# Two fused layers on one core: a norm pinned behind a multiplication, mixer factors issued sooner, down products moved, the last silu in halves

## The chip, the core and the metric

The kernel runs on one core of a Trainium2 chip. The metric is the device time of one execution in microseconds (us). Engines are named as the profile names them: PE (TensorE, matmuls) with PEld (its weight loads), DVE (VectorE), ACT (ScalarE), POOL (GpSimd) and SP (SyncE, which issues nearly all DMAs). Each engine works through its own queue in order, so an instruction that waits holds back all that stand behind it on that engine.

## What is computed

Four batches of 512 tokens with 256 features pass through two layers. Both layers compute `x + s * silu(ffn(xn))` with `xn = layernorm(x)`:

```
def ffn(x, W1, W2, W3):                 # H = 1024 hidden features
    hidden = silu(x @ W1.T) * (x @ W3.T)
    return fwht(hidden) @ W2.T          # fwht: normalised Hadamard transform
layer 0: s = xn + rmsnorm(mix(xn)) * norm_w      # mix starts from a zero state
layer 1: s = attention(layernorm(xn) * gamma + beta) + xn   # causal, one head
x = x + s * silu(ffn(xn))
```

Since the state of `mix` starts at zero, it is a linear map: the factors of B and C are summed to one number per feature, `g`, and `W_out`, `g` and `W_in` are multiplied to one 256x256 matrix `m` on the chip. The Hadamard transform is applied to W2 once per layer.

## The kernel before, in words

**Products.** All large products are made in three passes: each operand is split into a high part (a cast on ACT, line 61) and the rest (a subtraction on DVE, line 62), and PE multiplies high with high, high with low and low with high. `split` (line 59) is this pair of instructions. All matmuls go through line 70. In the profile, names ending in h and l are the two parts.

**Banks.** PE's results lie in eight PSUM banks in three groups: `gu` (3 banks), `dn` (2) and `ms` (3). A tile that is asked for takes the bank of its group that was given out longest ago, and its first product waits until the last reader of the former tile is done.

**Layer 0.** For each batch `ffn` (line 446) goes over eight chunks of 128 hidden features: two up products (`gu`, lines 484 to 502), silu on ACT (505), multiplication on DVE (506), a split (513). One chunk later `down` (456) multiplies by the transformed W2 into the two `dn` banks, which are given out at the start of `ffn` (452). Beside the chunks a list of background steps runs (`Beside`, line 832; each step ends at a `yield`). In batch 0 they are `prep_first` (919): the butterflies and products that transform W2 (`prep_w2`, 139), and `prep_m` (204), which makes `g` on DVE (lines 207, 209, 211), scales `W_out` by it on ACT (`wg`, line 214, four instructions), and multiplies (`mps`) to `m`; then the mixer (670). The order of the instructions in layer 0 is set by a planner that simulates a timeline before the run. `after(ins)` puts what is issued inside it behind `ins` on the same engine; it makes no wait between engines.

**Layer 1.** PE's order is written out by hand (`line["fixed"]`, line 1020): each matmul follows the one issued before it. The other engines are still planned. `ffn_s` (530) goes over four pairs of chunks, q = 0 to 3. For each it makes seven block products (Strassen's scheme) of six matmuls each, in the order gate, z, gate, z, gate, lin, gate, in three `gu` banks (`gate_`, `lin`, `z`). Between them stand eight places, filled from the list `places` by the caller (lines 1035 to 1063): steps of the attention (`sc`, `pt`, `pv`, `tq`, `v`), and numbers 0 to 3, which are the down products of the pair before: 0 and 1 for tokens 0 to 255 with the first and second chunk of the pair, 2 and 3 for tokens 256 to 511. `silu(h1)`, line 626 and a split make the hidden values of the first 256 tokens; `silu(h0)` (631), the multiplication at line 632 and a split (634 to 636) those of the other 256. Line 632 is the last reader of the pair's `lin` bank.

The next norm: at the last place of pair 3 of batches 0 and 1 the caller takes the first step of `norm(1, b + 2)` (412): means and variances on DVE (259, 261, 263), the power -1/2 on POOL (264), the scaling on DVE (266). It is issued inside `after(first["gate"])` (line 415); `first["gate"]` is, at that point, line 619 of the same pair, the addition to `v`. The second step, the moments of the normed values (`mr`, 243 to 248, again with a power on POOL), is issued at place 2 of the first pair of the next batch; at its place 7 PE transposes them (`mrp`) and they go to DRAM and back (`mrb`).

**The last batch.** Its down products for tokens 256 to 511 need two banks of `ms` beside the attention, so some of them stand as tuples in `places` (`later`, line 1058): `(q, chunk, (2, 3))` for tiles 2 and 3 of 128 tokens. What is left runs in the loop at 642, 36 matmuls, and `gate_tile` (1001) ends each tile with silu (1004), two DVE steps (1005, 1006) and a DMA (1007).

Of the kernel before, what the change touches and what calls it, by code (L numbers as in the profile page):

```python
# [17 lines left out]
ALU = mybir.AluOpType  # L18
# [17 lines left out]
def kernel(ctx: ExitStack, tc: tile.TileContext, a: dict, out: bass.AP):  # L36
# [142 lines left out]
    def product_of_weights(name, lhsT, rhs, nk, scale=None):  # L179

        hi = wp.tile([P, 2, D], F32R, name=f"{name}h")
        lo = wp.tile([P, 2, D], F32R, name=f"{name}l")
        o = psum(f"{name}ps", [P, 2, D])
        for i in range(2):
            for k in range(nk):
                matmul(
                    o[:, i, :], lhsT(k, i), rhs(k), start=k == 0, stop=k == nk - 1
                )
        if scale is None:
            split(o, hi, lo)  # L190
        else:
            nc.scalar.mul(hi, o, scale)
            nc.vector.scalar_tensor_tensor(lo, o, scale, hi.bitcast(F32), ALU.mult, ALU.subtract)
        return hi, lo
# [9 lines left out]
    def prep_m(win, wout):  # L204

        cb = wp.tile([P, 4, 2, DS], F32, name="cb")
        nc.vector.tensor_tensor(cb, bc[:, :, 0:2, :], bc[:, :, 2:4, :], ALU.mult)
        cbd = wp.tile([P, 4, DS], F32, name="cbd")
        nc.vector.tensor_tensor(cbd, cb[:, :, 0, :], cb[:, :, 1, :], ALU.subtract)
        g = wp.tile([P, 4], F32, name="g")  # L210
        nc.vector.tensor_reduce(g, cbd, AX.X, ALU.add)
        wg = t4("wg", [P, 4, D])
        for c in range(4):
            nc.scalar.mul(wg[:, c, :], wout[:, c, :], g[:, c : c + 1])
        return product_of_weights(
            "m", lambda k, i: win[:, k, i * P : (i + 1) * P], lambda k: wg[:, k, :], 4
        )

    def sl(i):
        return slice(i * P, (i + 1) * P)  # L220
# [60 lines left out]
        ]  # L281

    DN = {"tag": "dn", "bufs": 2}, {"tag": "ms", "bufs": 3}
    ALLS = slice(0, S)
    ALLD = slice(0, D)

# [159 lines left out]
    def ffn(name, xT, w13, w2, slot, defer=1, spare=(), parts=1, behind=False, tail=()):  # L446

        w2h, w2l = w2
        dn = [psum(f"{name}dn{i}", [P, 2, D], tag="dn", bufs=2) for i in range(2)]
        outs = [dn[t // 2][:, t % 2, :] for t in range(NT)]
        firsts = {}

        def down(c, hh, hl, tiles=range(NT)):
            for t in tiles:
                o = outs[t]
                for n, (l, r) in enumerate(((hh, w2h), (hh, w2l), (hl, w2h))):
                    first = c == 0 and n == 0  # L460
                    stop = c == NH - 1 and n == 2

                    def one(start):
                        return matmul(
                            o, l[:, sl(t)], r[:, c, :], start=start, stop=stop, skip_group_check=True
                        )

                    if first and t % 2 == 1:  # L470
                        with tc.issue_after(firsts[t // 2].ins):
                            ins = one(False)
                    elif first:
                        ins = firsts[t // 2] = one(True)
                    else:
                        ins = one(False)
            return ins

        queue, gates = [], []
        for c in range(NH):  # L480
            with after(gates[-2] if behind and c >= 2 else None):
                wh, wl = w13(c // 2)
            gu = []
            for j in range(2):
                o = psum(f"{name}gu{c}_{j}", [P, S], tag="gu", bufs=3)
                cols = slice((c % 2) * D + j * P, (c % 2) * D + (j + 1) * P)
                gu.append((o, cols))
            for half in range(parts if c == 0 else 1):
                n = S // (parts if c == 0 else 1)
                ts_ = slice(half * n, (half + 1) * n)  # L490
                if parts == 1 or c:
                    for o, cols in gu:
                        last_up = mm3(o[:, ts_], k_pairs((wh, wl), cols, xT, ts_))
                    continue

                for n, (w, x) in enumerate(((wh, xT[0]), (wl, xT[0]), (wh, xT[1]))):
                    for o, cols in gu:
                        for k in range(2):
                            last_up = matmul(
                                o[:, ts_], w[:, k, cols], x[:, k, ts_],  # L500
                                start=n + k == 0, stop=n + k == 3,
                            )
            gu = [o for o, _ in gu]
            h = hid(f"{name}h{c}")
            first["silu"] = nc.scalar.activation(h, gu[0], AF.Silu)  # L505
            gates.append(nc.vector.tensor_tensor(h, h, gu[1], ALU.mult))  # L506
            first["gate"] = gates[-1]
            if c < len(spare):
                hh, hl = spare[c]
            else:  # L510
                hh = hid(f"{name}hh{c}", F32R)
                hl = hid(f"{name}hl{c}", F32R)
            split(h, hh, hl)
            queue.append((c, hh, hl))
            ups = last_up if behind else None
            with after(gates[-1] if behind else None), after(ups):
                slot(2 * c)
            if len(queue) > defer:
                down(*queue.pop(0))
            with after(gates[-1] if behind else None), after(ups):  # L520
                slot(2 * c + 1)
        line["fixed"] = bool(tail)
        line["last"] = last_up
        for what in tail:
            what()
        for q in queue:
            down(*q)
        return dn

    def ffn_s(name, b, pairs, w2, beside, before, last=None):  # L530
# [45 lines left out]
        for q in range(NH // 2):  # L576
# [51 lines left out]
            split(h1, *hs[0])  # L628
            place(6)
            product(gate_, A22, T4, end=True)  # L630
            silu(h0, gate_)
            nc.vector.tensor_tensor(h0, h0, lin, ALU.mult)

            left.append(run(split, h0, *hs[1]))
            if q:
                left.pop()()
            hidden[q] = hs
            place(7)
            behind = units(q, hs)
        if last is None:  # L640
            return behind, dns
        for q, t in ((2, 2), (2, 3), (3, 0), (3, 1), (3, 2), (3, 3)):
            for c in range(2):
                down(q, c, hidden[q], (t,))
            if q == 3:
                last(t, outs[t])

    def gate(name, dn, s, x, store=None, halves=range(2)):
# [270 lines left out]
    def prep_first():  # L919
        steps = prep_w2(0, raw2, w2, x_slot)  # L920
        with after(first["w13"][1]):
            next(steps)
        yield
        for _ in range(4):
            next(steps)
            yield
        with after(first["silu"]):
            nc.scalar.copy(had, had_f)
        for _ in range(4):
            next(steps)  # L930
            yield
        load_x(1)
        first["m"] = prep_m(*raw_m)
        yield
        yield from steps

# [86 lines left out]
    for b in range(B):  # L1023
# [14 lines left out]
        if not final:  # L1038
            if b:
                places[0][2].append(run(next, norms[b + 1]))  # L1040
            places[0][7].append(run(next, norms[b + 1]))
            c = Attention(b + 1)
            tq, v_ = [run(c.tq, j) for j in range(2)], [run(c.v, 0, j) for j in range(2)]
            atts.append(c)
            places += [
                [[sc[2]], [sc[3], a.soft], [0], [pts[0]], [1, later_gates[0]], [pts[1], later_gates[1]], [2], [pv[0], pv[1], 3]],
                [
                    [pts[2]], [run(c.xt_half, 0)], [0, run(c.xt_half, 1), c.xt], [pv[2]],
                    [1, c.scaled], [pv[3]], [2, c.split_sums], [3],
                ],  # L1050
                [[tq[0]], [tq[1]], [0], [v_[0]], [1], [v_[1]], [2], [3]],
            ]
            if b + 2 < B:
                norms[b + 2] = norm(1, b + 2)
                places[3][7].append(run(next, norms[b + 2]))
            behind, dn = ffn_s(f"f1_{b}", b, pairs(b), w2_1, places, behind)
        else:
            later = [[(q, c, (2, 3)) for c in range(2)] for q in range(2)]
            places += [
                [[sc[2]], [sc[3], a.soft], [0], [pts[0]], [1, later_gates[0]], [pts[1], later_gates[1]], [], [pv[0], pv[1]]],  # L1060
                [[pts[2]], [pv[2], later[0][0]], [0], [pv[3]], [1], [later[0][1]], [], []],
                [[later[1][0]], [], [0], [], [1], [later[1][1]], [], []],
            ]
            ffn_s(f"f1_{b}", b, pairs(b), w2_1, places, behind, last=gate_tile)

# [67 lines left out]
```

## Time and profile before

| | |
|---|---|
| median of 3 runs | 368.06 us (367.82 to 368.28) |
| the profiled execution | 367.46 us |
| its span in the trace | 365.6 us |
| busy PE, DVE, ACT | 97%, 78%, 54% of the span |
| granted TensorE clock | 0.999 |
| layer 0, batch 0 | starts at 0, its products at 7.81 us |
| layer 1, first pair of batches 1 and 2 (z) | 222.43 and 270.59 us |
| start of the last matmul | 361.40 us |
| end of the last DVE step, issue of the last DMA | 363.1 and 363.13 us |

Times in the profile are counted from the start of the span. In a row of the timeline stand the start, the duration, the engine, the line, the operation, output and inputs with the shape, and in brackets how long the engine stood idle before it and which instruction ended that. In a row of waits stand the sum in us, how often, and the longest. A matmul of 256 columns lasts 0.28 us but the next one starts 0.12 us after it, so rows of PE overlap.

### The profile page before, as it was taken

The page shows a single profiled execution, that of the slowest core. Times are in us where ns is not written, and L with a number is a line of the kernel's source. Part 1 is how long each engine was busy: PE and PEld are TensorE (multiplying, and loading weights), DVE is VectorE, ACT ScalarE, POOL GpSimd, SP SyncE. Part 2 cuts the span into 40 slices and gives each one's busy share as a digit, 9 for nine tenths or more (in the row PEclk, how much of TensorE's full clock was granted, in tenths as well). Part 3 has the DMA queues.
Part 4 walks back from the last instruction along what each step waited for, and adds up shares of the span by engine and source line. Part 5 has one row for each costly group of instructions (what it writes and reads, how often), then busy time and mean ns, then how long its engine had stood idle before and what let it go on. Part 6 is the DMA issues. An engine that isn't in the chain of part 4 may idle for free.

```text
span 365.6 us, 6255 instructions
## 1 busy us (share of the span) xinstructions
PE 354.9 (97%) x2461; PEld 328.3 (90%) x2461; DVE 284.5 (78%) x600; ACT 195.9 (54%) x368; POOL 20.7 (6%) x22
## 2 busy tenths in 40 slices
PE   8999999999999999999999998999989999999995
PEld 6777998888988898889999998999989999999894
DVE  6998468997579938998787967989778897588445
ACT  4655427165363425663476744576555676556343
POOL 1000111100020210101100011000020000000000
PEclk9999999999999999999999999999999999999999
DMA  7925000405144326633065324761454635545301
GB/s 226 340 69 220 3 0 2 133 39 197 63 150 172 140 47 232 241 100 104 1 244 217 117 98 191 259 240 34 189 203 166 221 135 201 189 147 194 133 2 57
DMA packets 16284, 52.25 MB, mean 143 GB/s; under 512 B 1632, under 2 KB 7936, under 8 KB 16256
## 3 DMA queue, kind: packets, MB, share of 16 engines
q1 hardware_dynamic: 15968, 51.60, 39.9%
q8 instruction: 19, 0.31, 0.4%
q10 hardware_dynamic: 288, 0.26, 0.2%
q14 instruction: 9, 0.07, 0.1%
HBM read 42.40 MB, written 9.45 MB: 142 GB/s over the span
## 4 chain that ended last, share of the span: by engine, by line
PE 81%; DVE 10%; ACT 2%; DMA 2%; issue 2%; SPq 1%; POOL 1%; DVEq 0%
PE f_2dn L70 6%; PE f_1gu L70 6%; PE f_2gu L70 6%; PE f_3gu L70 6%; PE f_0dn L70 6%; PE f_1dn L70 6%; PE f_3dn L70 4%; PE sc L70 4%; PE pv L70 3%; PE o L70 3%; PE tq L70 3%; DMA w13raw<-in_w 2%; PE v L70 2%; PE pt L70 1%; PE mps L70 1%
## 5 line engine op out<-in xcount | busy, mean ns | idle before, releaser
L70 PE MATMUL f_3gu<-xt,w 128*128 128x512 f32 x96 | 25.0, 396 | 0.0
L70 PE MATMUL f_0gu<-xt,w 128*128 128x512 f32 (+1 forms) x108 | 24.5, 380 | 0.4 <-ACT f_0h L505 0.4
L70 PE MATMUL f_2gu<-xt,w 128*128 128x512 f32 x96 | 24.6, 395 | 0.0
L70 PE MATMUL f_1gu<-xt,w 128*128 128x512 f32 x96 | 24.4, 395 | 0.0
L70 PEld LDWEIGHTS f_0gu<-xt,w 128*128 128x128 f32 x108 | 18.4, 188 | 5.2 <-issue 1.0
L70 PEld LDWEIGHTS f_1gu<-xt,w 128*128 128x128 f32 x96 | 17.2, 188 | 3.3
L70 PEld LDWEIGHTS f_2gu<-xt,w 128*128 128x128 f32 x96 | 17.1, 188 | 3.2
L70 PEld LDWEIGHTS f_3gu<-xt,w 128*128 128x128 f32 x96 | 17.0, 188 | 2.9
L61 ACT CAST f_1hh<-f_1h 128x512 fp32r<-128x512 f32 x16 | 9.9, 621 | 16.1 <-DVE f_1h L506 12.1
L70 PE MATMUL f_3dn<-w2h,f_3hh 128*128 128x256 f32 x64 | 17.8, 283 | 0.7 <-DVE pl L62 0.7
L61 ACT CAST f_2hh<-f_2h 128x512 fp32r<-128x512 f32 x16 | 9.9, 622 | 16.0 <-DVE f_2h L506 12.6
L70 PE MATMUL f_1dn<-w2l,f_1hh 128*128 128x256 f32 x64 | 17.9, 284 | 0.0
L70 PE MATMUL f_3dn<-w2l,f_3hh 128*128 128x256 f32 x64 | 17.7, 281 | 0.0
L70 PE MATMUL f_1dn<-w2h,f_1hh 128*128 128x256 f32 x64 | 17.7, 281 | 0.0
L70 PE MATMUL f_2dn<-w2h,f_2hh 128*128 128x256 f32 x64 | 17.7, 282 | 0.0
L70 PE MATMUL f_2dn<-w2l,f_2hh 128*128 128x256 f32 x64 | 17.6, 281 | 0.0
L70 PE MATMUL f_3dn<-w2h,f_3hl 128*128 128x256 f32 x64 | 17.1, 283 | 0.2 <-DVE f_3hl L62 0.2
L70 PE MATMUL f_1dn<-w2h,f_1hl 128*128 128x256 f32 x64 | 17.2, 282 | 0.0
L61 ACT CAST f_3hh<-f_3h 128x512 fp32r<-128x512 f32 x16 | 9.9, 621 | 12.7 <-DVE f_3h L506 7.9
L70 PE MATMUL f_2dn<-w2h,f_2hl 128*128 128x256 f32 x64 | 16.7, 281 | 0.0
L62 DVE TENSOR_TENSOR f_3hl<-f_3h,f_3hh 128x512 fp32r<-128x512 f32 x16 | 11.0, 686 | 4.1 <-ACT f_3hh L61 4.0
L62 DVE TENSOR_TENSOR f_2hl<-f_2h,f_2hh 128x512 fp32r<-128x512 f32 x16 | 10.9, 683 | 4.2 <-ACT f_2hh L61 4.1
(469 smaller groups left out, 1137.8 us busy)
## 6 DMA issues: line engine op xcount, KB each, us to landing
sw<-s SPq DMA_DIRECT2D x32, 896.0 KB, 4.8
s<-sp SPq DMA_DIRECT2D x8, 512.0 KB, 3.3
s<-sp SPq DMA_DIRECT2D x8, 384.0 KB, 4.2
w2raw<-in_w SPq DMA_DIRECT2D x4, 512.0 KB, 5.7
sraw<-in_w SPq DMA_DIRECT2D x4, 512.0 KB, 4.7
mrb<-there SPq DMA_DIRECT2D x4, 512.0 KB, 4.2
w13raw<-in_w SPq DMA_DIRECT2D x3, 512.0 KB, 7.7
x<-in_x SPq DMA_DIRECT2D x3, 512.0 KB, 3.5
```

Source lines behind the costliest of these rows:

```text
L61: h = nc.scalar.copy(hi, src)
L62: return h, engine.tensor_tensor(lo, src, hi.bitcast(F32), ALU.subtract)
L70: ins = call(*args, **kwargs)
```

## The change

1. `first["gate"]` is now also set by the multiplication at line 632, so that the next norm stands behind it on DVE.
2. `prep_m` gets a `yield` before its product. Its first part, the three DVE instructions for `g` and the four ACT instructions for `wg`, is issued two steps sooner; the product stays where it was.
3. In batch 0 the up products of chunk 1 take the two `dn` banks, not two of `gu`; in all batches of layer 0 the `dn` tiles of the down products are asked for at the first down product.
4. In the last batch the units 0 and 1 and the tuples of `later` change places in pairs 2 and 3.
5. In the last pair of the last batch silu, multiplication and split of the last 256 tokens are made in two halves of one chunk each, and the order of the closing products is by chunk for tiles 2 and 3.

```diff
@@ prep_m
+        yield
+        first["m"] = product_of_weights(
             "m", lambda k, i: win[:, k, i * P : (i + 1) * P], lambda k: wg[:, k, :], 4
         )
+        yield
...
@@ ffn
-        dn = [psum(f"{name}dn{i}", [P, 2, D], tag="dn", bufs=2) for i in range(2)]
-        outs = [dn[t // 2][:, t % 2, :] for t in range(NT)]
-        firsts = {}
+        dn, outs, firsts = [], [], {}
         def down(c, hh, hl, tiles=range(NT)):
+            if not dn:
+                dn.extend(psum(f"{name}dn{i}", [P, 2, D], tag="dn", bufs=2) for i in range(2))
+                outs.extend(dn[t // 2][:, t % 2, :] for t in range(NT))
...
-                o = psum(f"{name}gu{c}_{j}", [P, S], tag="gu", bufs=3)
+                o = psum(f"{name}gu{c}_{j}", [P, S], **(DN[0] if behind and c == 1 else GU))
...
@@ ffn_s
             product(gate_, A22, T4, end=True)
+            hidden[q] = hs
+            if last is not None and q == NH // 2 - 1:
+                for c in range(2):
+                    silu(h0[:, c, :], gate_[:, c, :])
+                    nc.vector.tensor_tensor(h0[:, c, :], h0[:, c, :], lin[:, c, :], ALU.mult)
+                    split(h0[:, c, :], *(z[:, c, :] for z in hs[1]))
+                break
             silu(h0, gate_)
-            nc.vector.tensor_tensor(h0, h0, lin, ALU.mult)
+            first["gate"] = nc.vector.tensor_tensor(h0, h0, lin, ALU.mult)
...
-        for q, t in ((2, 2), (2, 3), (3, 0), (3, 1), (3, 2), (3, 3)):
-            for c in range(2):
-                down(q, c, hidden[q], (t,))
-            if q == 3:
+        for q, c, t in (
+            (2, 0, 2), (2, 1, 2), (2, 0, 3), (2, 1, 3), (3, 0, 0), (3, 1, 0), (3, 0, 1), (3, 1, 1),
+            (3, 0, 2), (3, 0, 3), (3, 1, 2), (3, 1, 3),
+        ):
+            down(q, c, hidden[q], (t,))
+            if (q, c) == (3, 1):
                 last(t, outs[t])
...
@@ prep_first
-        for _ in range(4):
+        for _ in range(2):
+            next(steps)
+            yield
+        product = prep_m(*raw_m)
+        next(product)
+        for _ in range(2):
             next(steps)
             yield
         load_x(1)
-        first["m"] = prep_m(*raw_m)
+        next(product)
         yield
...
@@ places of the last batch, pairs 2 and 3
-                [[pts[2]], [pv[2], later[0][0]], [0], [pv[3]], [1], [later[0][1]], [], []],
-                [[later[1][0]], [], [0], [], [1], [later[1][1]], [], []],
+                [[pts[2]], [pv[2], 0], [], [pv[3]], [1], [later[0][0]], [], [later[0][1]]],
+                [[later[1][0]], [later[1][1]], [], [0], [], [1], [], []],
```

More of the change, by code (lines that the diff above doesn't have):

```diff
@@ L214, in prep_m @@
             nc.scalar.mul(wg[:, c, :], wout[:, c, :], g[:, c : c + 1])
-        return product_of_weights(
+        yield
+        first["m"] = product_of_weights(
             "m", lambda k, i: win[:, k, i * P : (i + 1) * P], lambda k: wg[:, k, :], 4
         )
+        yield
     def sl(i):
@@ L283 @@
     DN = {"tag": "dn", "bufs": 2}, {"tag": "ms", "bufs": 3}
+    GU = {"tag": "gu", "bufs": 3}
     ALLS = slice(0, S)
@@ L636, in ffn_s @@
                 left.pop()()
-            hidden[q] = hs
             place(7)
```

## The prediction

> **What bounds the kernel now.** I read the page's busy times first, then the waits of TensorE (who waited for whom, us in total), then the timeline around each wait, then the chain that ended last.
>
> ```profile
> PE 354.9 (97%) x2461; PEld 328.3 (90%) x2461; DVE 284.5 (78%) x600; ACT 195.9 (54%) x368; POOL 20.7 (6%) x22
> ```
>
> PE works for 354.9 of 365.6 us. The change removes no product, so it can gain only in PE's pauses and in the 3.9 us after the last product. These are PE's waits:
>
> ```profile
> PE f_2gu0z L70 <- DVE f_1h L632: 1.3, 1, 1.3
> PE f_1gu0z L70 <- DVE f_0h L632: 1.3, 1, 1.3
> PE f_3dn L70 <- DVE pl L62: 0.7, 1, 0.7
> PE mps L70 <- ACT wg L214: 0.7, 1, 0.7
> PE f_3gu3z L70 <- DVE f_3h L632: 0.6, 1, 0.6
> PE f_0gu L70 <- ACT f_0h L505: 0.4, 1, 0.4
> PE f_3dn L70 <- DVE f_3hl L62: 0.2, 1, 0.2
> ```
>
> A wait costs more than its row, because a running matmul's end is counted as busy. By the starts of single matmuls, 256 columns normally follow each other in 0.12 us and 512 in 0.23. The matmul before f_1gu0z starts at 220.82, f_1gu0z at 222.43 and its second at 222.65: 1.49 too late and 0.10 more for a cold start, 1.6 us. Likewise f_2gu0z is 1.6, f_3dn 0.98, mps 0.95 (29.74 to 30.84), f_3gu3z 0.85, f_0gu 0.65 (14.05 to 14.83), the last f_3dn 0.5. Sum 7.1 us: the most that the change can take from PE.
>
> **The pinned norm** (timeline, batch 0 into 1: start, us, what):
>
> ```profile
> 214.73 1.40 DVE L259 BATCH_NORM_STATS2 ln_2st<-x 128x6 f32<-128x256 f32 x4
> 217.73 1.38 POOL L264 TENSOR_TENSOR ln_2r<-ln_2r,mhalf 128x4 f32<-128x4 f32 x1 [40.97 <-DVE ln_2r L263]
> 218.80 0.59 ACT L573 ACTIVATE f_0h<-f_0gu3g 128x512 f32<-128x512 f32 x1
> 219.15 1.38 DVE L266 TENSOR_SCALAR xn<-x,ln_2mv,ln_2r 128x256 f32<-128x256 f32 x4 [0.90 <-POOL ln_2r L264]
> 220.44 0.68 DVE L62 TENSOR_TENSOR f_0hl<-f_0h,f_0hh 128x512 fp32r<-128x512 f32 x1
> 221.71 0.67 DVE L632 TENSOR_TENSOR f_0h<-f_0h,f_0gu3l 128x512 f32<-128x512 f32 x1
> 222.43 0.97 PE L70 MATMUL f_1gu0z<-tb,sw 128*128 128x256 f32 x6 [1.33 <-DVE f_0h L632]
> ```
>
> L632 frees the bank of lin that z of the next batch takes. Its silu is ready at 219.4, yet DVE stands 0.90 us for POOL's power and then runs the norm's xn ahead of it. With the pin the norm is behind L632. The gate's last product ends at 218.26 (217.39 + 0.87), silu 0.59, then the multiplication: 218.9 to 219.6. Z is due at 220.94, so both pauses of 1.6 go, 3.2 us.
>
> Where the stall goes: the norm starts 4.9 us later (219.6, not 214.7), and PE's written order has mrp, which transposes the moments, at 231.03. Before, the moments were ready at 225.8 (POOL 224.78 + 1.01), 5.1 us early. PE now gets there 1.6 sooner: due 229.3. New chain: bn_stats 1.3, aggregates and the eps 0.5 with one split of 0.6 between (222.0), power (223.4), xn 1.3 (224.7), second bn_stats and aggregates 1.75 (226.5), up to three of FFN and gate at 0.6 each between them (228.3), power 1.0 (229.3). Just in time. Bounds: with none between it is 0.7 to 1.8 early and the 3.2 stay; if two more come between, 1.2 late twice. I take 0.2 late twice: **2.8 us**. L622, which the sixth product waits for, has 1.1 us to spare (ends 228.38, product's weights at 229.50); two bn_stats ahead of it (0.33 each) fit. The norm issues no DMA; the moments' two go through SP with mrp, and mrb lands in 4.2 us, at about 241.5, for a use at 248.0.
>
> [...] the same 128x4 power took 1.01 at 224.78 with DVE idle, 1.38 at 217.73 beside L626 (both inputs in SBUF). By the idle row both powers together are 2.0[...]. I use 2.4, 1.4 for the first and 1.0 for the second[...]. [...] by the idle row they are 0.4 sooner and it is 3.2.
>
> **The head: mixer's factors and the up products' banks.** DVE has no gap there (windows: length, PE, PEld, DVE), and mps waits for it through ACT:
>
> ```profile
> 22.00:30.80 8.80, 8.14 (x35) 6.18 (x33) 8.78 (x16) 4.05 (x8) 0.00 (x0) 1.00 0.40 123
> 29.98 0.21 DVE L211 TENSOR_REDUCE g<-cbd 128x4 f32<-128x64 f32 x1
> 30.28 1.71 ACT L214 ACTIVATE wg<-wout,g 128x256 f32<-128x256 f32 x4 [2.33 <-issue]
> ```
>
> The factors are issued two steps sooner: three DVE instructions that follow in 0.2 + 0.14 + 0.13 = 0.47 us, and four on ACT (1.71), which sat idle 0.9 before 25.89. The weights they need landed by 16.4, long before. So g comes near 24.5 and wg by 26.5, 4 us ahead of PE's 30.0: 0.95 gained. What they push back: DVE's queue by up to 0.47, ACT's cast of w2bh by up to 0.8 (w2ps runs at 31.2, hidden), a silu queued behind wg by up to 1.7, where its bank has about 1 us of slack. Bound: +0.95 to -0.5; I take 0.9. No DMA moves past another; load_x(1) stays between the same steps.
>
> Chunk 1 in the dn banks takes away the wait for a bank at 14.83 (0.65), since dn is first written at 36.54. But DVE was busy 4.24 of 4.40 us up to 14.8 and without a gap from there to 30.7, and at 27.64 PE loads its weights 0.06 us after DVE's split of w (26.37 + 1.22) is done. A PE that is ahead meets that split and gives the time back. Bound 0 to 0.65; I take 0.1, since that split is the nearest row. **Head 1.0 us.** Allocating dn later in the other batches costs nothing: no PE wait lies between 31 and 220.
>
> **The tail of batch 3** (timeline):
>
> ```profile
> 338.97 0.68 DVE L62 TENSOR_TENSOR pl<-pt,ph 128x512 fp32r<-128x512 f32 x1
> 339.71 0.39 PE L70 MATMUL f_3dn<-w2h,f_3hh 128*128 128x256 f32 x1 [0.72 <-DVE pl L62]
> 350.17 0.98 PE L70 MATMUL f_3gu3z<-tb,sw 128*128 128x256 f32 x6 [0.59 <-DVE f_3h L632]
> 359.48 0.69 DVE L62 TENSOR_TENSOR f_3hl<-f_3h,f_3hh 128x512 fp32r<-128x512 f32 x1 [0.69 <-ACT f_3hh L61]
> 360.23 0.39 PE L70 MATMUL f_3dn<-w2h,f_3hl 128*128 128x256 f32 x1 [0.23 <-DVE f_3hl L62]
> ```
>
> Tile 3's first down product takes its ms bank only after pl. Moved to the fifth place it finds it free; the unit put in its stead writes dn banks, needs a split done at 338.45 and starts at 338.47; the z after it (339.2) needs L632, done at 339.05. So 0.98 goes, perhaps 0.1 stays. In pair 3 two blocks of six (0.71 each) now stand before z where one stood, and in pair 2 one more after the third gate product: 7 blocks, 4.97 us, from that product's end to z, against 4.15 from 346.02 to 350.17. So 0.85 goes. PE's closing 36 down products then start at 354.8 of the old clock, not 356.6.
>
> Halves: in 512 columns silu, multiplication, cast and split take 0.59, 0.68, 0.62, 0.69; in 256, by gate_tile's rows, about 0.38, 0.42, 0.38, 0.42. Started in a row and shifted by 1.8 to 2.0, the second half's split ends near 357.7 (before: 360.17). PE comes to the first half at 357.65 and to the second at 358.36, so 0.5 goes too. [...] At the very end tiles 2 and 3 finish three products apart, not six: 0.35 less room between two gates, whose DVE steps are 0.42 each; 0.3 is given back. 2.33 - 0.3 gives 2.0 to 2.1; bounds 1.2 and 2.3: **2.0 us**.
>
> **Sum.** 2.8 + 1.0 + 2.0 = 5.8. The profiled execution took 367.46, its span 365.6; this makes it 361.7. The median is 368.06, 0.6 above it: 362.3.
>
> **Rivals.**
> - The wait moves to mrp (0.13): [...] DVE puts more between, so the moments come 1.2 to 1.6 late in both batches. It speaks for it that the estimate has no slack. The norm then gives 0 to 0.8: 3.0 to 3.8 in all, 364.3 to 365.1.
> - DVE and ACT stay the bound (0.10): head nothing, tail only its first two waits less the 0.3, 1.2: 4.0 in all, 364.1. The gapless DVE speaks for it; against it, g is last in a queue for which nothing else waits.
> - Slower (0.05): the norm keeps its old length of 11.1 us (214.7 to 225.8) and L632 stays near its old end of 222.4, because of silus and casts queued ahead on ACT. The moments then come at 233.5 and PE waits 2.5 at mrp beside the old 1.6, twice: 5.0 lost against 3.0 gained, 370.1. Against it: ACT is busy 2.14 of the 5.20 us before 219.2. It decides once mrp is over 1.5 us later than in the trace.
> - The change doesn't bite (0.03): layer 0 is planned anew and opens new pauses of some 3 us, while the norm only moves its wait: 368.
>
> The first case has 0.69 and 361 to 363.5. A measurement of this kernel can tell about 0.2% (0.7 us) from no change. The range reaches from all pauses gone (361.0) to the two first rivals' mean.
>
> **What would show it.** L632 before bn_stats, and no PE wait at f_1gu0z and f_2gu0z; mrp without a wait, or with it at POOL's mr; wg done before 28; no f_0gu wait near 14.8 but perhaps one near 27; no wait at f_3dn behind pl or at f_3gu3z; the last product's start, 361.40 before, near 355.3. A PE wait above 1 us at mrp, or a new one in layer 0, would prove me wrong.

## The result and the profile after

The changed kernel takes 373.32 us (372.6 to 373.76) against 367.94 for the kernel before in the same runs: a ratio of 1.0145, 95% interval 1.0122 to 1.0167. It is slower by 5.4 us; 362.3 was forecast. The profiled execution took 372.6 us, its span is 370.8 and its granted clock 0.991. The page's busy times, and PE's waits (who waited for whom, us in total, times, longest):

```profile
PE 357.1 (96%) x2461; PEld 330.0 (89%) x2461; DVE 285.8 (77%) x602; ACT 196.0 (53%) x370; POOL 19.9 (5%) x22
```

```profile
PE mrp L70 <- POOL mr L250: 6.3, 2, 3.1
PE warm L70 <- DVE zr L900: 1.5, 1, 1.5
PE f_2gu2z L70 <- DVE f_2h L645: 0.6, 1, 0.6
PE f_1gu2z L70 <- DVE f_1h L645: 0.6, 1, 0.6
PE f_0gu L70 <- ACT xt L404: 0.2, 1, 0.2
PE f_0gu L70 <- DVE w L62: 0.2, 1, 0.2
PE f_0gu L70 <- DVE f_0h L511: 0.2, 1, 0.2
```

The seven waits shown of the kernel before are gone (warm, the start's filler products, stood there too), and one new pair outweighs them: PE stands 3.1 us at mrp, the transposition of the moments, in each of the two batches. Lines moved: 632 is now 645, 619 is 624, the powers 264 and 248 are 266 and 250. The starts of some matmuls show where the time goes (us from the start of the span):

| first matmul of | before | after | difference |
|---|---|---|---|
| layer 0's products | 7.81 | 8.22 | +0.41 |
| batch 1 (f_1gu) | 53.29 | 53.09 | -0.20 |
| z behind the first norm (f_1gu0z) | 222.43 | 220.72 | -1.71 |
| mrp, first | 231.03 | 232.51 | +1.48 |
| f_1gu2z | 244.88 | 247.03 | +2.15 |
| z behind the second norm (f_2gu0z) | 270.59 | 271.25 | +0.66 |
| mrp, second | 279.16 | 283.03 | +3.87 |
| f_2gu2z | 293.00 | 300.15 | +7.15 |
| the last product | 361.40 | 366.29 | +4.89 |
| end of the span | 365.65 | 370.82 | +5.17 |

Z gains 1.5 in each batch (at the first, 1.71 less the 0.20 that the head brought; 1.6 was forecast), and from z to mrp PE loses 3.2 each time. The timeline of DVE and POOL between the two, with PE's first z and mrp (start, us, what; in brackets the idle time before and what ended it):

```profile
219.17 0.68 DVE L645 TENSOR_TENSOR f_0h<-f_0h,f_0gu3l 128x512 f32<-128x512 f32 x1
219.76 1.40 DVE L261 BATCH_NORM_STATS2 ln_2st<-x 128x6 f32<-128x256 f32 x4
222.68 0.17 DVE L265 TENSOR_SCALAR ln_2r<-ln_2mv 128x4 f32<-128x4 f32 x1
224.53 0.69 DVE L624 TENSOR_TENSOR f_1v<-f_1gu0z,f_1v 128x512 f32<-128x512 f32 x1 [1.68 <-PE f_1gu0z L70]
225.14 1.37 DVE L268 TENSOR_SCALAR xn<-x,ln_2mv,ln_2r 128x256 f32<-128x256 f32 x4
227.35 0.68 DVE L674 TENSOR_TENSOR g_0g<-g_0g,xn 128x512 f32<-128x512 f32 x1
229.22 0.66 DVE L675 TENSOR_TENSOR x<-x,g_0g 128x512 f32<-128x512 f32 x1
231.14 0.16 DVE L249 TENSOR_SCALAR mr<-ln_2mv 128x4 f32<-128x4 f32 x1
```

```profile
222.92 1.01 POOL L266 TENSOR_TENSOR ln_2r<-ln_2r,mhalf 128x4 f32<-128x4 f32 x1 [46.34 <-DVE ln_2r L265]
231.45 1.01 POOL L250 TENSOR_TENSOR mr<-mr,mhalf 128x4 f32<-128x4 f32 x1 [7.52 <-DVE mr L249]
```

```profile
232.51 0.27 PE L70 MATMUL mrp<-ident,mr 128*8 128x128 f32 x1 [3.13 <-POOL mr L250]
247.03 0.71 PE L70 MATMUL f_1gu2z<-tb,sw 128*128 128x256 f32 x4 [0.57 <-DVE f_1h L645]
```

L645 is first and the power is done at 223.93. But the norm's scaling (L268) starts only at 225.14: DVE stood 1.68 us in front of L624, which waits for PE's z, and the scaling was queued behind it. From there DVE has no gap. The moments' last DVE step starts at 231.14, their power ends at 232.46, and PE had been due at 229.22: mrp is 3.3 late, in both batches. The windows of DVE's busy time (length, then PE, PEld, DVE, ACT, POOL, clock) show the exchange: the first two rows are of the kernel before, the other two of the changed one:

```profile
212.00:219.00 7.00, 7.00 (x62) 7.00 (x61) 4.19 (x14) 2.53 (x5) 1.27 (x1) 1.00 0.03 11
224.50:231.30 6.80, 6.80 (x60) 6.78 (x59) 4.41 (x12) 2.44 (x4) 1.01 (x1) 1.00 0.09 30
```

```profile
224.50:231.30 6.80, 4.88 (x42) 4.68 (x40) 6.77 (x23) 2.01 (x4) 0.00 (x0) 1.00 0.26 71
212.00:219.00 7.00, 7.00 (x62) 7.00 (x61) 3.12 (x5) 2.80 (x5) 0.00 (x0) 1.00 0.08 13
```

Work was taken out of a stretch in which DVE had 2.8 us to spare (now 3.9) and put where it had 2.4 to spare (now none).

### The profile page after: what moved, and what is told of

Its sections match the earlier page's. It is cut to its first block, busy times and chain, and to the rows that moved or that the text cites. A ratio compares the mean times of both kernels' runs of the same rounds, so it can differ in the third digit from the quotient of the medians.

```text
span 370.8 us, 6257 instructions
## 1 busy us (share of the span) xinstructions
PE 357.1 (96%) x2461; PEld 330.0 (89%) x2461; DVE 285.8 (77%) x602; ACT 196.0 (53%) x370; POOL 19.9 (5%) x22
## 4 chain that ended last, share of the span: by engine, by line
PE 87%; DVE 7%; ACT 2%; DMA 1%; issue 0%; SPq 0%; POOLq 0%; POOL 0%; DVEq 0%
PE f_1gu L70 6%; PE f_2gu L70 6%; PE f_3gu L70 6%; PE f_3dn L70 6%; PE f_2dn L70 6%; PE f_0dn L70 6%; PE f_1dn L70 5%; PE f_0gu L70 5%; PE sc L70 4%; PE pv L70 3%; PE o L70 3%; PE v L70 3%; PE tq L70 3%; DMA w13raw<-in_w 1%; PE w2ps L70 1%; PE pt L70 1%
## 5 line engine op out<-in xcount | busy, mean ns | idle before, releaser
L70 PE MATMUL f_0gu<-xt,w 128*128 128x512 f32 (+1 forms) x108 | 25.3, 382 | 0.6 <-ACT xt L404 0.2
L61 ACT CAST f_3hh<-f_3h 128x512 fp32r<-128x512 f32 (+1 forms) x17 | 10.0, 595 | 12.1 <-DVE f_3h L511 7.9
L62 DVE TENSOR_TENSOR f_3hl<-f_3h,f_3hh 128x512 fp32r<-128x512 f32 (+1 forms) x17 | 11.0, 654 | 3.6 <-ACT f_3hh L61 3.3
```

The source lines that it names most:

```text
L61: h = nc.scalar.copy(hi, src)
L62: return h, engine.tensor_tensor(lo, src, hi.bitcast(F32), ALU.subtract)
L70: ins = call(*args, **kwargs)
```

## The experiments

Times are medians, with the ratio to the kernel before in the same runs and its 95% interval. "Late" is how much later than the normal spacing a matmul starts.

**pin_alone**: the kernel before with part 1 only.

```diff
-            nc.vector.tensor_tensor(h0, h0, lin, ALU.mult)
+            first["gate"] = nc.vector.tensor_tensor(h0, h0, lin, ALU.mult)
```

> The kernel before with only the pin (first["gate"] set by the multiplication that ends pair 3). Theory A (the pin makes the moments late and PE stands at mrp in its written order): 1.7 us gained at f_1gu0z and f_2gu0z each, 3.3 lost at mrp each, about 0.6 more at gu2z each, and 2.6 from a colder clock after the second pause: 368 + 7.4 = 375, at least 371 if the clock holds. Rival B (the other edits changed the plan, and that made mrp late): the pin alone gains its 3 us, 365.

375.41 us, 1.0213 (1.0190 to 1.0236). Its waits begin with the same row, and the old waits of head and tail stand beside it:

```profile
PE mrp L70 <- POOL mr L248: 6.3, 2, 3.1
PE f_2gu2z L70 <- DVE f_2h L632: 0.6, 1, 0.6
PE f_1gu2z L70 <- DVE f_1h L632: 0.6, 1, 0.6
```

One line of the change makes all of the loss.

**all_but_pin**: the changed kernel without that line.

```diff
-            first["gate"] = nc.vector.tensor_tensor(h0, h0, lin, ALU.mult)
+            nc.vector.tensor_tensor(h0, h0, lin, ALU.mult)
```

> The changed kernel without the pin. Theory A: the head's 0.2 and the tail's 2.0 are left: 365.7, pauses of 1.5 at f_1gu0z and f_2gu0z back, mrp without a wait. Rival B: mrp still waits about 3 us in batches 1 and 2, over 370.

364.99 us, 0.9924 (0.9910 to 0.9937). The two waits at z are back, none is at mrp; the span is 2.4 shorter than before, 0.4 of it from the head. The other four parts are worth 2.7 us by the medians.

```profile
PE f_1gu0z L70 <- DVE f_0h L645: 1.3, 1, 1.3
PE f_2gu0z L70 <- DVE f_1h L645: 1.3, 1, 1.3
```

**mrp_later**: mrp moved from place 7 of the first pair to place 2 of the second, with the norm as late as in the change.

```diff
-            places[0][7].append(run(next, norms[b + 1]))
+            if not b:
+                places[0][7].append(run(next, norms[b + 1]))
...
+            if b:
+                places[1][2].append(run(next, norms[b + 1]))
```

> The changed kernel, but in batches 1 and 2 mrp (with its copy and its two DMAs) stands at place 2 of the second pair, about 4.6 us later in PE's order. Theory A: no wait at mrp (moments at 232.5, mrp at 233.9), so the pin's 3.2 us are kept: 362.5, or 363.8 if the 0.6 at gu2z stays. Rival C (the late norm itself fills DVE and delays the FFN's own chain): the time goes to other PE waits, over 367. The mean and scale come back 4 us later and are then about 1.7 us early for their use; if that fails, a wait of ACT and DVE at xf shows.

365.40 us, 0.9934 (0.9922 to 0.9947): 2.9 above the expected 362.5. The wait at mrp is gone, but there is a new one, 1.65 late in each batch:

```profile
PE f_1gu1z L70 <- DVE f_1h L645: 1.5, 1, 1.5
PE f_2gu1z L70 <- DVE f_2h L645: 1.5, 1, 1.5
```

Now the multiplication of the next pair is late. It is not only mrp that is too early: DVE as a whole is behind.

**norm_early**: the norm's first step at place 2 of pair 3 instead of 7, where it stands behind L645 of pair 2.

```diff
-                places[3][7].append(run(next, norms[b + 2]))
+                places[3][2].append(run(next, norms[b + 2]))
```

> The changed kernel, but the norm's first step is issued at place 2 of pair 3 (not at place 7), behind the multiplication that ends pair 2, so it is done before pair 3 needs DVE. Theory A: neither f_1gu0z nor mrp waits: 362 to 363. Rival C (DVE lacks the room for the norm in this stage): the norm's 4.8 us push the pair's multiplication or L624 back, and f_1gu0z waits 1 us or more: over 365.

362.77 us, 0.9867 (0.9853 to 0.9880). No wait at mrp. The rest at z, 0.3, comes from the moments, which are not pinned and were now planned ahead of L645.

**early_two_pins**: the same, with the moments pinned behind L645 of pair 3.

```diff
-            moments(f"ln2_{b}", xn, mr)
+            with after(first["gate"] if b > 1 else None):
+                moments(f"ln2_{b}", xn, mr)
```

> The run norm_early with one thing more: the moments of batches 2 and 3 are issued behind the multiplication that ends pair 3, so they can't stand ahead of it. Theory A: the 0.54 at f_1gu0z and f_2gu0z that norm_early kept goes: 362.8 - 1.1 = 361.7, with no wait at mrp, which has 5 us to spare. Rival: the moments then meet the full stage of DVE and mrp or f_1gu1z waits: 363 or more.

361.97 us, 0.9842 (0.9827 to 0.9856), the fastest of all. These are all its waits; none is in layer 1. Below them, DVE around L646 (the same multiplication):

```profile
PE warm L70 <- DVE zr L901: 1.5, 1, 1.5
PE f_0gu L70 <- DVE f_0h L512: 0.4, 1, 0.4
PE f_0gu L70 <- DVE w L62: 0.2, 1, 0.2
```

```profile
214.32 1.38 DVE L268 TENSOR_SCALAR xn<-x,ln_2mv,ln_2r 128x256 f32<-128x256 f32 x4
218.99 0.68 DVE L646 TENSOR_TENSOR f_0h<-f_0h,f_0gu3l 128x512 f32<-128x512 f32 x1
219.59 1.40 DVE L245 BATCH_NORM_STATS2 ln_2st<-xn 128x6 f32<-128x256 f32 x4
222.98 0.16 DVE L249 TENSOR_SCALAR mr<-ln_2mv 128x4 f32<-128x4 f32 x1
```

The moments' power ends at 224.30; mrp runs at 229.04 without a wait. PE is 3.57 earlier than before at f_2gu2z, of which 0.40 is the head: 3.17 from the norm, the 3.2 of the forecast's wait.

**xn_first**: the changed kernel, with L624 of the next batch's first pair behind the norm's scaling. (The name in the edit is set anew for each 128 tokens, so L624 stands behind the last of the four; the trace has it there.)

```diff
-                nc.vector.tensor_scalar(
+                first["scaled"] = nc.vector.tensor_scalar(
...
-            first["gate"] = nc.vector.tensor_tensor(v, z, v, ALU.add)
+            with after(first["scaled"] if q == 0 and b in (1, 2) else None):
+                first["gate"] = nc.vector.tensor_tensor(v, z, v, ALU.add)
```

> The changed kernel, but in the first pair of batches 1 and 2 the addition to v stands behind the norm's scaling on DVE, not ahead of it, so DVE doesn't wait for z before it scales. Theory E (a good part of the delay is DVE standing 1.7 us behind that addition): the moments come 0.7 to 1.2 sooner, mrp waits 1.9 to 2.4[...]: 368.5 to 369.5. Rival F (what lies between the later steps sets the moments): no gain, 373.

**gate_later**: the changed kernel, with the gate's multiplication of the batch before (L674) behind the moments' eps.

```diff
-        nc.vector.tensor_scalar(mr[:, 1, :], mv[:, :, 1], LN_EPS, None, ALU.add)
+        first["moments"] = nc.vector.tensor_scalar(mr[:, 1, :], mv[:, :, 1], LN_EPS, None, ALU.add)
...
-                nc.vector.tensor_tensor(g, g, s[:, ts_, :], ALU.mult)
+                with after(first["moments"] if store is not None else None):
+                    nc.vector.tensor_tensor(g, g, s[:, ts_, :], ALU.mult)
```

> The changed kernel, but the gate's multiplications of the batch before (0.6 each, with their additions) stand behind the moments on DVE in batches 1 and 2. Theory F (the steps of other work that the plan puts between the norm's own set the delay): the moments come about 1.2 sooner, mrp waits 1.9, the clock stays up: 368.5. Rival E alone: 373. The gate's stores leave later, which nothing waits for.

xn_first: 371.07 us, 1.0084 (1.0061 to 1.0106); mrp is late by 2.46 and 2.47 instead of 3.29 and 3.30, so the place behind L624 is worth 0.83: DVE stands 1.12 us in front of the scaling instead of 1.68 in front of L624, but L624 itself still runs ahead of the moments. gate_later: 368.80 us, 1.0027 (1.0010 to 1.0044), from 366.82 to 370.50; mrp is late by 2.08, so L674 and L675 are worth 1.21, and the wait at the last z of the next pairs is gone. Both times say less than the traces, since in either profiled run the clock fell to 0.50 behind both pauses, of 2.3 us in xn_first and of 1.9 in gate_later (see keep_warm and the last section); gate_later's expectation had the clock stay up.

**both_first**: the changed kernel with both pins.

> The changed kernel with two pins more: z's addition to v behind the norm's scaling of the first 128 tokens, and the gate's multiplication of batch b behind the moments' eps. Apart, the first made the lateness at mrp 0.83 us smaller in each batch and the second 1.21. If the two are separate terms (theory E with F), the lateness falls from 3.30 to 1.2 to 1.4 and what is left is the norm's late start itself; the wait at the last z of pair 0 stays away. With the clock up throughout, 370.8 of span less 2 x 2.04, less 2 x 0.8 for that z, less 2.6 for the slow products is 362.5, about 364.5 as a time; with the clock falling in one batch 367. Rival: they are not separate, since the second pin fills the same DVE time in which the first one waits: lateness 1.8 to 2.1 and 366.5 to 369, no better than the second alone.

365.95 us, 0.9952 (0.9939 to 0.9966). mrp is late by 1.55 and 1.57, where 3.30 - 0.83 - 1.21 gives 1.26. The missing 0.3 is in one row: the power took 1.32 here, beside the multiplication that was put behind the eps. That multiplication (L676) starts 0.2 before the power.

```profile
228.71 0.16 DVE L249 TENSOR_SCALAR mr<-ln_2mv 128x4 f32<-128x4 f32 x1
228.78 0.68 DVE L676 TENSOR_TENSOR g_0g<-g_0g,xn 128x512 f32<-128x512 f32 x1
```

```profile
229.01 1.32 POOL L250 TENSOR_TENSOR mr<-mr,mhalf 128x4 f32<-128x4 f32 x1 [5.47 <-PE f_0dn L70]
```

So the two are separate terms, and 1.26 of the 3.3 is in neither of them. The time is 1.4 above the expected 364.5: 0.6 is the power in two batches, the rest was not followed.

**keep_warm**: the changed kernel with twelve products more ahead of mrp in each of the two batches, into the same bank; their result is overwritten.

```diff
+            whole = psum(f"mrp{b}", [P, S])
+            if b > 1:
+                for _ in range(12):
+                    matmul(whole, w2_1[0][:, 0, :P], w2_1[0][:, 0:2, :].rearrange("p a d -> p (a d)"), start=True, stop=True)
```

> The changed kernel with twelve extra products of 512 columns (2.8 us, their result is overwritten) in front of mrp in batches 1 and 2, so that PE works through most of the pause there. Theory A (the slow products from 283 to 289 us come from a clock that the 3 us pause lets drop): mrp is as late as before, but the products after it keep their pace and the granted clock stays near 0.999: 373.3 - 2.6 = 370.7. Rival D (they are slow for another reason, such as the traffic of that stage): 373.

369.74 us, 1.0054 (1.0039 to 1.0069), although mrp comes as late as before (232.21 and 282.76): PE was busy while it waited, and that saved 3.6 us of the median (2.9 between the two profiled executions). The window behind the second mrp, first the changed kernel and then this one (the number in round brackets behind PE's time is its matmuls, 0.50 and 1.00 the granted clock):

```profile
283.50:289.00 5.50, 5.50 (x19) 4.95 (x18) 2.91 (x6) 3.06 (x8) 0.00 (x0) 0.50 0.77 293
```

```profile
283.50:289.00 5.50, 5.50 (x41) 5.24 (x40) 4.59 (x12) 3.64 (x10) 0.00 (x0) 1.00 0.82 290
```

In the same 5.5 us PE does 19 matmuls at half clock and 41 at full clock.

**factors_alone** and **banks_alone**: the kernel before with part 2 alone and with part 3 alone (diffs as in the change).

> The kernel before with the second part of the change alone: the mixer's factors g and wg two steps sooner, the product mps where it was. The forecast gave it 0.9 us (the wait of 0.7, 0.95 with its cold start, at mps behind wg). Theory H: that wait goes, but DVE has no gap up to 30.7 us and PE is ahead of it only so long as another DVE result is not late, so only 0.2 to 0.5 us arrive behind the head: 367.4 to 367.7 (before 367.8 to 367.9 in the runs so far), with a new small wait of PE at a chunk's split. Rival I: the whole 0.9 arrives, 366.9 to 367.0, and what the changed kernel's head lacks was lost by the banks' part.

> The kernel before with the third part alone: chunk 1's up products in the two dn banks, the dn tiles asked for at the first down product. Theory H: the wait of 0.4 (0.65 late) near 14.8 us goes, PE then meets DVE's split of w near 27.6 and gives it back, the wait at mps stays 0.7 or grows: 0 to 0.1 us gained, 367.8, the same as before. Rival I: it costs time in the head, 0.3 to 0.5 us, since DVE's order is planned anew around it: 368.2 to 368.3. Rival J: the 0.65 arrives in full: 367.2.

factors_alone: 367.12 us, 0.9982 (0.9975 to 0.9989), between the times of the two theories. mps waits no more (1.06 with its cold start), but f_0gu's wait for ACT near 14.8 grew from 0.4 to 0.8 and a late start came at 24.8: 0.4 is left at f_1gu. banks_alone: 367.94 us, 1.0004 (0.9996 to 1.0013). The 0.66 near 14.8 is gone; six late starts between 23 and 29 (0.99 in all), among them one at DVE's split of w, and a mps wait 0.13 longer take more than that, and PE is 0.46 late at f_1gu. How far single traces settle such amounts is said under "The head". First a row of factors_alone, then two of banks_alone:

```profile
PE f_0gu L70 <- ACT f_0h L507: 0.8, 1, 0.8
```

```profile
PE mps L70 <- ACT wg L214: 0.8, 1, 0.8
PE f_0gu L70 <- DVE w L62: 0.2, 1, 0.2
```

**no_halves**: early_two_pins without the halves of part 5; the closing order stays.

```diff
-            if last is not None and q == NH // 2 - 1:
-                for c in range(2):
-                    silu(h0[:, c, :], gate_[:, c, :])
-                    nc.vector.tensor_tensor(h0[:, c, :], h0[:, c, :], lin[:, c, :], ALU.mult)
-                    split(h0[:, c, :], *(z[:, c, :] for z in hs[1]))
-                break
```

> The version with both norm steps pinned and started sooner (361.97), less the fifth part's halves: the last silu, multiplication and split of batch 3 in 512 columns again, the closing products still in the new order (by chunk for tiles 2 and 3). The forecast gave the halves 0.5 less 0.3. If its step is right, PE waits again 0.2 (0.5 late) before the closing products of the last 256 tokens: 362.2 to 362.5. Rival K: since the moved down products already let z start 1.8 us sooner, the wait is longer than before, 0.8 to 1.0 late, as DVE's split of 512 columns comes after PE: 362.8 to 363.0. Rival L: it makes nothing, 361.9 to 362.1.

362.52 us, 0.9857 (0.9843 to 0.9870). The old last wait is back, and only that:

```profile
354.74 0.39 PE L70 MATMUL f_3dn<-w2h,f_3hl 128*128 128x256 f32 x1 [0.23 <-DVE f_3hl L62]
```

From the first of the closing 36 products to the last it takes 4.72 us here, as in the kernel before, and 4.17 with the halves: 0.55, forecast 0.5. So the halves bring it, and the closing order alone brings nothing here.

## Why the prediction was wrong, point by point

**The step that failed** is "Where the stall goes", with its "0.2 late twice". Its sum let the norm's chain go on at once wherever its input was ready, with only one split and three FFN or gate steps of 0.6 between its links; the wait of other work in the queue ahead of the chain was not in it. So the moments were to come just as PE does, and they came 3.2 later. Its own points against the trace:

| | forecast | measured |
|---|---|---|
| L632 (645) done | 219.6 | 219.85 |
| eps of the first power done | 222.0 | 222.85 |
| first power done | 223.4 | 223.93 |
| scaling starts | 223.4 | 225.14 |
| moments' last DVE step done | 228.3 | 231.30 |
| second power done | 229.3 | 232.46 |

The lateness of 3.2 has three large terms: one more split of 0.6 ahead of the eps; 1.2 for L624, in front of which DVE stood for PE's z while the scaling was ready behind it; and 1.2 for other work of 3.0 between scaling and moments (L627, L674, L675, L631 at 0.6 each, two masks and a reduction at 0.2) instead of "up to three" at 0.6. The rest nearly cancels: the start 0.25 later, the first power 0.4 shorter than assumed, the second's start 0.15 after its input. xn_first took the standing of the second term away and won 0.83, gate_later took L674 and L675 out of the third and won 1.21, both_first won both. The split was not tested alone. The forecast's bound, "1.2 late twice", was far too near. The prediction nowhere counts DVE's free time in the stretch to which the norm moves: 2.4 us of 6.8. Small slips of its sum don't matter beside this: PE's due time is 231.03 less 1.6, 229.4 and not 229.3, and its range ends at 363.5, while the two first rivals' mean is 364.4.

The rival that ended slower had the place and the sign: it put the wait at mrp and its turning point at 1.5 us later than in the trace. Its cause was wrong (L632 did not stay near 222.4) and so was its size: 2.5 beside the old 1.6, against 3.3 without it. It got 0.05.

**Two prices were in no case.** After the second pause the granted clock was 0.50 for the products behind it, about 2.6 us net (from mrp to z of the third pair PE takes 17.12 us, and 14.52 behind the first pause), and DVE's backlog reaches the next pair but one: f_1gu2z and f_2gu2z wait 0.6 for L645, and start 0.6 later behind their forerunners than in the kernel before.

**Right: the waits at z.** Both are gone, 1.5 us each. early_two_pins brings the 3.2 home, so the benefit was read rightly and its price was not.

**The powers.** Both took 1.01, not 1.4 and 1.0: when the first started DVE ran nothing, when the second started a reduction had 0.18 left, and a split began 0.1 later. In both_first L676 was running when the second power started, and it took 1.32. The rows show more: where a multiplication or a split was running on DVE when the power started, the power ended some 0.87 after that instruction's end. In the kernel before, L626 with 0.51 left goes with a power of 1.38, and a split of 128x1024 at 106.33 with 1.05 left goes with 1.91; in both_first L676 with 0.45 left goes with 1.32. (The power at 119.60 in the kernel before does not fit: 1.17 with 0.16 left.) The split that began 0.1 after the power's start cost nothing: 1.01. That it matters whether an input lies in SBUF was not shown.

**The head, 1.0 forecast, 0.6 measured** between the profiled executions (counted from the first product, which itself starts 0.41 later). Both waits went, 1.7 with cold starts, and six late starts of 0.1 to 0.33 between 23 and 29 took 1.1 back; for the two longest the profile names DVE, as the forecast's bound for the banks had it. g came at 28.4 and not at 24.5, and wg ended at 30.4 against mps at 30.76, so "4 us ahead" was wrong. It is the same step as at mrp: the three DVE instructions for g were to follow each other in 0.47, but their last two start 2.5 us apart already in the kernel before (27.5 and 29.98) and 4.3 apart in the changed one (24.1 and 28.42), with other work of the queue between.

One trace settles a head only to some 0.3 us. pin_alone has the layer 0 of the kernel before, in the same order, and takes 45.80 from the first product to f_1gu where the kernel before takes 45.48 (changed 44.87, factors_alone 45.10, banks_alone 45.92). The silu near 14.8 stands on ACT behind a cast that waits for a DMA of weights, and that landed 0.2 later. First the kernel before, then pin_alone:

```profile
13.23 1.05 ACT L61 CAST w<-w13raw 128x1024 fp32r<-128x1024 f32 x1 [1.42 <-DMA w13raw<-in_w]
13.45 1.05 ACT L61 CAST w<-w13raw 128x1024 fp32r<-128x1024 f32 x1 [1.74 <-DMA w13raw<-in_w]
```

factors_alone's longer wait there has the same cause (13.57). So the head brought 0.6 to 0.9. By the medians the factors alone bring 0.7 and the banks alone nothing clear of noise; that the two depend on each other is not shown.

**Right: the tail.** From f_2gu2z to the last product PE gains 2.26 (7.15 to 4.89; forecast 2.33) and to the end 1.98 (forecast 2.0). No wait of PE is left there (the moved units of part 4 were not run alone); the halves run as expected, each in about 0.38:

```profile
363.56 0.74 DVE L641 TENSOR_TENSOR f_3h<-f_3h,f_3gu3l 128x256 f32<-128x256 f32 x2
364.44 0.76 DVE L62 TENSOR_TENSOR f_3hl<-f_3h,f_3hh 128x256 fp32r<-128x256 f32 x2
```

The sum in the trace: -0.2 to f_1gu, +1.7 to the first mrp, +0.7 to f_1gu2z, +1.7 to the second mrp, +3.3 to f_2gu2z, -2.0 to the end: 5.2 in all.

**Open.** What kept early_two_pins' last 0.6 at f_0gu was not followed.

## What to carry to other kernels

Putting work behind an instruction moves the whole chain that hangs on it; before pinning, count the free time of the engine in the stretch where the chain will lie, and every instruction between its links, those that wait for another engine first. A consumer in a fixed order (here mrp) is a deadline: if the producer is moved later, start the chain earlier by as much, as early_two_pins does, or the stall only changes its address. A pause of PE may cost more than its length, by the clock behind it: here 1.4 us did not (1.00 behind it) and 1.9 us did (0.50), while of two pauses of 3.1 us in one run only the second did. So a time with such a pause scatters from run to run: gate_later's from 366.82 to 370.50.

## What the runs showed of the hardware

**The granted clock fell to 0.50 after some pauses of PE and not after others.** In the profiled runs it stayed at 1.00 after the pauses of 1.4 us in both_first and after the first of 3.1 us in the changed kernel; it fell after the second there, after both of 2.3 in xn_first and after both of 1.9 in gate_later. The traces show a pattern in this. A fall lasts 3.41 us (each one in xn_first and gate_later), or twice that (6.83 in the changed kernel), and the falls of one run lie whole multiples of 3.41 apart: xn_first's at 232.34 and 283.54 (15 times 3.41), the changed kernel's at 282.13 and, behind its last product, at 370.88 (26 times). Windows of 3.41 us laid back from 282.13 tell its two equal pauses apart (the third number from the right is the clock):

```profile
227.52:230.93 3.41, 1.86 (x16) 1.66 (x15) 3.41 (x13) 0.99 (x2) 0.00 (x0) 1.00 0.42 97
230.93:234.34 3.41, 1.83 (x13) 1.83 (x14) 3.38 (x10) 2.69 (x5) 1.01 (x1) 1.00 1.00 397
278.72:282.13 3.41, 1.17 (x10) 0.97 (x9) 3.41 (x16) 1.10 (x3) 0.17 (x1) 1.00 0.54 189
282.13:285.54 3.41, 2.51 (x11) 2.52 (x12) 3.27 (x7) 2.58 (x7) 0.84 (x1) 0.50 0.99 365
285.54:288.95 3.41, 3.41 (x10) 2.91 (x9) 1.01 (x3) 1.05 (x4) 0.00 (x0) 0.50 0.68 250
```

The first pause lies across a border of this grid: PE stands 1.55 us in one window and 1.58 in the next, and the clock stays up. Of the second, 2.24 us lie in one window, and the clock is at half from that window's end. In the next window PE stands another 0.90, and the clock stays at half for one more, in which PE never stands. In gate_later the whole pause of 1.9 lies in one window, and one window at half follows:

```profile
228.01:231.42 3.41, 1.50 (x14) 1.29 (x13) 3.41 (x15) 1.71 (x4) 1.01 (x1) 1.00 0.61 200
231.43:234.84 3.41, 3.41 (x14) 3.31 (x13) 2.82 (x6) 2.34 (x6) 0.00 (x0) 0.50 0.98 397
```

Laid over all profiled runs, the grid fits every pause behind the first product: up to 1.75 us of standing in a window (pin_alone's first pause) left the clock at 1.00, 1.91 (gate_later's first) and more halved it. What lies between is unknown, and no run moved a pause against the grid on purpose. The grid does not lie at the same place in all of them: gate_later's first fall begins at 231.42, xn_first's at 232.34. The runs of one kernel differ too: gate_later's 20 fall into three groups, 366.82 to 367.05 us at a mean clock of 0.998, 368.45 to 368.81 at 0.993 to 0.995, and 369.98 to 370.50 at 0.990 or 0.991. That fits none, one and two falls of 1.7 us each (an estimate: half of 3.41, at a clock of 0.50); the profiled run, 370.08, had two.
